# Splitting a projection step around the values, and adding a bias one unit later, in a fused cross-attention and FFN kernel

## The chip, the cores and the metric

The kernel runs on one core of a Trainium2 chip. The metric is the device time of one execution in microseconds (us). Five engines work on it side by side, each with its own queue in order: TensorE (PE in the profile, with its weight loads as PEld), VectorE (DVE), ScalarE (ACT), GpSimd (POOL) and SyncE (SP), which only issues DMAs here. Engines wait for one another by semaphores.

## The reference

Inputs are x and ctx of shape (4, 1024, 512), the projection weights of an attention with 16 heads of 32 columns, their biases, and three weight matrices of a gated feed-forward block that is computed with fake quantisation.

```
q  = layernorm(x) @ Wq + bq;  k = ctx @ Wk + bk;  v = ctx @ Wv + bv      # 16 heads of 32
scores = q k^T / sqrt(32), masked:
    image rows (the first 768) attend within their own block of 256
    text rows (the last 256) attend to all image columns, causally to text columns
x1  = x + softmax(scores) @ v @ Wo + bo
xq  = int8 fake quantisation of layernorm(x1), one scale for the whole tensor
h   = silu(xq @ quant(w_gate)^T) * (xq @ quant(w_up)^T)
out = x1 + quantised(h) @ quant(w_down)^T
```

All is fp32 to the outside; the attention's products are fp32 and the feed-forward's are bf16 of integer values.

## The kernel before, in words

The attention comes first (about 887 us), then the feed-forward block (about 250 us). The change is in the attention alone.

Each batch has four blocks of 256 queries: three image blocks and one text block. The unit of work is one block, one group of four heads and one block of 256 keys: a class `Unit`. An image block has 4 units (one part each); a text block has 16, with four parts per group. That makes 112 units. A loop over n takes them in a software pipeline written out by hand, and the order of instructions on PE, DVE, ACT and POOL is the order of this code (`manual_schedule`). Iteration n holds, for TensorE:

- `maxima`: the scores s of unit n, two PSUM tiles of two banks each, from which VectorE takes maxima;
- `large`: one projection step (`big_step`, a part of a q, k or v projection: names pp_q, pp_kv, pv) or one step of the output's projection (`step_output`, name po). A step is four products over the 128-row parts of the contraction, each in four column groups of 32 (`column_groups`). It writes one bank of a pool with one buffer (`ps_mm`, tag mm), which must be emptied before the next step: by ScalarE for pp and pv, by VectorE for po (`Output.take`);
- `weights` of unit n - 5 (`T_LAG`): the shifted scores t into two PSUM tiles, and two exp of ScalarE, one for each tile, into pT (two buffers). On POOL follow the causal mask (`affine_select`) and the running sums sp of pT over keys;
- `values` of unit n - 6 (`V_LAG`): pT times v into av; after a block's last part also the sums, sp times ones, into the same bank (L548), whose result ScalarE copies out.

s and t share one pool of three buffers (`ps_sc`, tag sc). So the second tile of s takes the buffer that the first exp of the unit before has read.

Some iterations before `LATE` (n = 84) hold a second `big_step` at their end; from `LATE` on the steps are halved. Work that is to be done a little later stands in two lists: `later`, which is run in the next iteration after `large`, and `background`, of which one entry is taken in each iteration.

`Output` is the output's projection of a block. `load` fetches x into xr (two buffers) and puts `add_bias` into `later`; `add_bias` adds bo_b to it on POOL; `take` adds po to xr on VectorE, calling `add_bias` first if that has not been done, and after the second half stores xr to x1_d by a DMA that POOL issues. `tail` is the `Output` of the last block, whose `load` is called from `values_now`.

`output_bias` makes bo_b = bo + bv @ Wo once, on all partitions: `spread` copies bv over 128 columns and `product` runs four full-size products into one bank. They are called at n = 2 and n = 4.

Of the kernel before, what the change touches and what calls it, by code (L numbers as in the profile page):

```python
# [10 lines left out]
F32 = mybir.dt.float32  # L11
# [8 lines left out]
P = 128  # L20
# [22 lines left out]
def kernel(ctx: ExitStack, tc: tile.TileContext, x, kv, Wq, bq, Wk, bk, Wv, bv, Wo, bo, clip_x, clip_down, w_gate, w_up, w_down, out):  # L43
# [78 lines left out]
    with ExitStack() as actx:  # L122
# [65 lines left out]
        def output_bias():  # L188

            bvr = wk2.tile([P, NCC, P], F32, tag="wst", name="bvr", bufs=1)  # L190

            def spread():
                nc.vector.tensor_copy(bvr, bqk[:, 2 * NCC :].unsqueeze(2).to_broadcast([P, NCC, P]))

            def product():
                pb = ps_sc.tile([P, 2, 2, QB], F32, tag="sc", name="pbo").rearrange("p a b c -> p a (b c)")[:, 0, :]
                for cc in range(NCC):
                    nc.tensor.matmul(pb, bvr[:, cc, :], W["Wo"][:, cc, :], start=(cc == 0), stop=(cc == NCC - 1))
                nc.vector.tensor_tensor(bo_b, pb, bo_b, ALU.add)

            return spread, product

# [41 lines left out]
        class Job:  # L244
# [32 lines left out]
            def rows(self, dst, w, b, scale, co, parts):  # L277

                pk = bank(f"pp_{self.kind}_{self.c}_{co}_{parts[0]}").rearrange("p (a q) -> p a q", a=2)
                for a in parts:  # L280
                    for ci in range(NCC):
                        lhs = W[w][:, ci, (co + a) * P : (co + a + 1) * P]
                        column_groups(pk[:, a, :], lhs, self.T[:, ci, :], ci == 0, ci == NCC - 1)
                for a in parts:
                    bias = bqk[:, b + co + a : b + co + a + 1]
                    nc.scalar.activation(dst[:, co + a, :], pk[:, a, :], AF.Identity, bias=bias, scale=scale)

# [17 lines left out]
            def run_big(self, half=False):  # L305

                parts = (self.part,) if half or self.part else (0, 1)
                c, i = self.c, self.big
                first = parts[0] == 0
                if self.kind == "q":  # L310
                    if i == 0 and first:
                        Q[c] = qp.tile([P, NCC, QB], F32, tag="qT", name=f"qT_{c}")
                    self.rows(Q[c], "Wq", 0, QK_SCALE, 2 * i, parts)
                elif i < 2:
                    if i == 0 and first:
                        K[c] = kp.tile([P, NCC, QB], F32, tag="kT", name=f"kT_{c}")
                    self.rows(K[c], "Wk", NCC, 1.0, 2 * i, parts)
                else:
                    i -= 2
                    if i == 0 and first:  # L320
                        V[c] = kp.tile([P, 2, C], F32, tag="va", name=f"va_{c}")
                    cols = slice(parts[0] * QB, (parts[-1] + 1) * QB)
                    pv = bank(f"pv_{c}_{i}_{parts[0]}")
                    for ci in range(NCC):
                        column_groups(pv[:, cols], self.T[:, ci, i * P : (i + 1) * P], W["Wv"][:, ci, cols], ci == 0, ci == NCC - 1)
                    nc.scalar.copy(V[c][:, i, cols], pv[:, cols])
                if parts[-1] == 1:
                    self.big += 1
                    self.part = 0
                else:  # L330
                    self.part = 1
                return len(parts)

# [143 lines left out]
        def weights(u, between):  # L477
# [16 lines left out]
            pT = wk2.tile([P, 4, 2, QB], F32, tag="pT", name=f"pT_{u.n}")  # L494
            for h in range(2):
                nc.scalar.activation(pT[:, 2 * h : 2 * h + 2], prs[h], AF.Exp)  # L496
                if h == 0:
                    between()
            if diag:

                for n in range(2):
                    d = pT[:, :, n, n * P : (n + 1) * P]
                    nc.gpsimd.affine_select(out=d, in_=d, compare_op=ALU.is_ge, fill=0.0, base=0, pattern=[[0, 4], [1, P]], channel_multiplier=-1)
            u.pT = pT

            if u.direct:
                return
            if u.part == 0:
                state["sum", k.n, g] = wk2.tile([P, 4, QB], F32, tag="sp", name=f"sp_{u.n}")
            sp = state["sum", k.n, g]  # L510
            for n in range(2):
                cols = slice(P, QB) if diag and n else slice(0, QB)
                if u.part == 0 and n == 0:
                    continue
                a = pT[:, :, 0, :] if u.part == 0 else sp[:, :, cols]
                nc.gpsimd.tensor_tensor(sp[:, :, cols], a, pT[:, :, n, cols], ALU.add)  # L516

# [52 lines left out]
        class Output:  # L570
# [5 lines left out]
            def load(self):  # L576
                if self.xr is None:
                    self.xr = load_block(x_tok, self.k.c, "xr", bufs=2)
                    later.append(self.add_bias)

# [24 lines left out]
            def step(self, half=False):  # L605
                i = self.i
                cols = slice(self.part * QB, (self.part + 1) * QB) if half or self.part else slice(0, C)
                po = ps_mm.tile([P, 512], F32, tag="mm", name=f"po_{self.k.n}_{i}_{self.part}")
                for cc in range(NCC):
                    column_groups(po[:, cols], self.k.oT[:, cc, i * P : (i + 1) * P], W["Wo"][:, cc, cols], cc == 0, cc == NCC - 1)  # L610
                statistics = self.take(po, i, cols)
                if statistics is None:
                    self.part = 1
                else:
                    background.appendleft(statistics)
                    self.part = 0
                    self.i += 1

# [82 lines left out]

        def big_step(half=False):
            nonlocal at_big, spent
            j = jobs[at_big]
            spent += BIG * j.run_big(half) / 2
            rows_done[j.kind[0], j.c] = min(2 * j.big + j.part, NCC)
            if j.big == j.bigs:
                done.add((j.kind[-1], j.c))
                at_big += 1

        def advance(n):
# [23 lines left out]

        def step_output(half=False):
            outputs[0].step(half)
            if outputs[0].i == 2:
                outputs.pop(0)
                for o in outputs[:2]:  # L740
                    o.load()

# [5 lines left out]
        def large(n):  # L748

            if n < LATE:  # L750
                if outputs and (len(outputs) > 1 or spent + BIG >= target(n)):
                    step_output()
                elif can_big(n) and spent < target(n):
                    big_step()
                elif outputs:
                    step_output()
                elif can_big(n) and spent < target(n) + 3 * BIG:
                    big_step()
                else:
                    return False  # L760
            elif can_big(n):
                big_step(n < len(units))
            elif outputs:
                step_output(n < len(units))
            else:
                return False
            return True
# [49 lines left out]
        early[0] = False  # L817
        spread, product = output_bias()
        for n in range(len(units) + V_LAG):
            previous = units[n - 1] if 0 < n <= len(units) else None  # L820
            if n < len(units):
# [6 lines left out]
                if u.part == u.parts - 1:  # L828
                    minus_maxima(u)
            if n in (2, 3, 4):  # L830
                (spread, sigmoids, product)[n - 2]()
            f = background.popleft() if background and n > 0 else None
            if f is not None and f.__name__ in ("deviation", "apply", "quantise"):
                f()
                f = background.popleft() if background and f.__name__ == "quantise" else None
            full = large(n)
            fs = list(later)
            later.clear()
# [5 lines left out]
            def shifts_of_previous():  # L844
                if previous is not None and previous.part == previous.parts - 1:
                    shifts(previous)

            def weights_now():
                if T_LAG <= n < len(units) + T_LAG:
                    weights(units[n - T_LAG], shifts_of_previous)  # L850
                else:
                    shifts_of_previous()

            def values_now():
# [4 lines left out]
                if u.part == u.parts - 1 and u.g == 0:  # L859
                    while len(outputs) >= OUTS:  # L860
                        step_output()
                if u is units[-4]:
                    tail.load()
                return values(u)

            if full:
                weights_now()
                ends = values_now()
            else:
                ends = values_now()  # L870
                weights_now()
            if n == len(units) + V_LAG - 2:
# [332 lines left out]
```

## Time and profile before

| what | value |
|---|---|
| median of 3 runs | 1138.64 us (1138.23 to 1140.09) |
| the profiled execution's own time | 1139.15 us |
| its span, first to last instruction | 1137.4 us |
| mean granted TensorE clock | 0.992 of full speed |
| PE busy | 1116.0 us, 98% of the span |
| DVE, ACT, POOL busy | 784.9, 500.1, 551.5 us |
| HBM over the span | 92 GB/s |

How to read it: the busy time of an engine is the union of its instructions' spans. Ends of matmuls are modelled, so a stall of a fraction of a microsecond inside a group of matmuls shows only in the distance from one start to the next. In a timeline line the columns are start, duration, engine, line, operation, what it writes and reads, shapes, count, and in brackets the idle time before it with what ended it.

### The profile page before, as it was taken

The numbers are of one execution on the slowest core, as the hardware profiler recorded it, in microseconds if no ns is written. First come the engines' busy times: TensorE is split into PE (matmuls) and PEld (weight loads), VectorE is DVE, ScalarE is ACT, GpSimd is POOL, SyncE is SP. The second block draws the span as 40 slices with busy tenths as digits, with TensorE's granted clock in tenths as the row PEclk, the third lists the DMA queues.
The fourth block names the chain that finished last, engine by engine and source line by source line (L and its number), as shares of the span: only waits on it lengthen the run. The fifth ranks groups of instructions, "written<-read, shape, count | busy, mean of one in ns | idle before, by whom it ended". The sixth has DMA issues, their size and how long they took to land.

```text
span 1137.4 us, 31369 instructions
## 1 busy us (share of the span) xinstructions
PE 1116.0 (98%) x13811; PEld 562.5 (49%) x13833; DVE 784.9 (69%) x979; ACT 500.1 (44%) x700; POOL 551.5 (48%) x618
## 2 busy tenths in 40 slices
PE   9999999999999999999999999998999899998998
PEld 5545545455545445454545455555554344444344
DVE  2545776766577857567777765875667788877887
ACT  3234433343444424344433445543333465553553
POOL 1224556577664567775556568657753222110110
PEclk9999999999999999999999999999999899999999
DMA  8342213133222222331312122111311599320895
GB/s 260 109 123 74 62 43 108 47 88 93 80 62 76 79 84 63 95 101 34 92 67 73 56 76 73 37 49 27 106 61 62 164 291 268 69 38 28 290 386 194
DMA packets 117201, 119.09 MB, mean 105 GB/s; under 512 B 55548, under 2 KB 86536, under 8 KB 115656
## 3 DMA queue, kind: packets, MB, share of 16 engines
q1 hardware_dynamic: 111104, 83.26, 26.3%
q0 software_dynamic: 5648, 33.30, 7.6%
q8 instruction: 108, 1.77, 0.7%
q10 hardware_dynamic: 312, 0.53, 0.2%
q14 instruction: 29, 0.24, 0.1%
HBM read 71.57 MB, written 33.29 MB: 92 GB/s over the span
## 4 chain that ended last, share of the span: by engine, by line
PE 91%; DVE 3%; DMA 2%; POOL 2%; ACT 1%; issue 1%; DVEq 0%; POOLq 0%; ACTq 0%
PE pv L219 10%; PE po L219 9%; PE pp_kv L219 9%; PE pp_q L219 9%; PE av L530 9%; PE t L491 8%; PE pg L1045 7%; PE pu L1045 7%; PE s L439 6%; PE s L428 5%; PE t L486 3%; PE av L548 3%; PE pd L1148 2%; DMA xt<-x_d 2%; POOL sp L516 2%
## 5 line engine op out<-in xcount | busy, mean ns | idle before, releaser
L496 ACT ACTIVATE pT<-t 128x1024 f32<-128x1024 f32 x224 | 217.1, 1021 | 190.2 <-PE t L491 160.1
L516 POOL TENSOR_TENSOR sp<-sp,pT 128x1024 f32<-128x1024 f32 x86 | 191.7, 2229 | 39.1 <-ACT pT L496 35.6
L450 DVE TENSOR_REDUCE nmh<-s 128x2 f32<-128x1024 f32 (+1 forms) x128 | 145.3, 1156 | 67.3 <-PE s L439 65.1
L516 POOL TENSOR_TENSOR sp<-pT 128x1024 f32<-128x1024 f32 x59 | 139.9, 2372 | 87.9 <-ACT pT L496 87.7
L432 DVE TENSOR_REDUCE nmh<-s 128x4 f32<-128x1024 f32 x96 | 112.8, 1216 | 97.7 <-PE s L428 95.5
L219 PE MATMUL pp_q<-qT,Wq_sb 128*32 128x256 f32 x2048 | 119.3, 383 | 0.0
L530 PE MATMUL av<-pT,va 128*32 128x256 f32 (+1 forms) x1792 | 116.5, 377 | 1.0 <-ACT avs L893 1.0
L219 PE MATMUL pv<-Wv_sb,kvT 128*32 128x512 f32 (+1 forms) x1088 | 116.9, 570 | 0.0
L491 PE MATMUL t<-qT,kT 32*128 32x256 f32 (+1 forms) x1792 | 113.4, 367 | 0.0
L219 PE MATMUL po<-Wo_sb,oT 128*32 128x512 f32 (+1 forms) x1120 | 110.3, 534 | 0.3
L563 DVE RECIPROCAL avs<-avs 128x256 f32<-128x256 f32 x63 | 109.8, 1742 | 0.0
L219 PE MATMUL pp_kv<-kvT,Wk_sb 128*32 128x256 f32 x1920 | 109.6, 380 | 0.0
L564 POOL TENSOR_TENSOR oT<-avs 128x256 f32<-128x256 f32 x63 | 45.9, 729 | 98.1 <-DVE avs L563 98.0
L491 PEld LDWEIGHTS t<-qT,kT 32*128 32x128 f32 x1792 | 88.3, 185 | 7.0
L1045 PE MATMUL pg<-xqT,wgT 128*128 128x512 bf16 x344 | 90.2, 382 | 1.1 <-DVE xqT L1006 0.5
L1045 PE MATMUL pu<-xqT,wuT 128*128 128x512 bf16 x345 | 90.2, 382 | 0.4
L1051 ACT ACTIVATE silu<-pg,sg 128x512 f32<-128x512 f32 x88 | 60.0, 686 | 65.6 <-PE pg L1045 63.5
L219 PEld LDWEIGHTS pp_q<-qT,Wq_sb 128*32 128x32 f32 x2048 | 63.7, 110 | 48.8 <-issue 8.7
L1072 DVE SCALAR_TENSOR_TENSOR h<-pu,su,silu 128x512 f32<-128x512 f32 x88 | 65.4, 747 | 30.9 <-PE pu L1045 28.3
L219 PEld LDWEIGHTS pp_kv<-kvT,Wk_sb 128*32 128x32 f32 x1920 | 60.1, 110 | 44.1 <-issue 5.4
L439 PE MATMUL s<-kT,qT 32*128 32x256 f32 (+1 forms) x1024 | 76.4, 387 | 3.2 <-ACT pT L496 3.2
L530 PEld LDWEIGHTS av<-pT,va 128*32 128x32 f32 x1792 | 46.8, 109 | 54.5 <-issue 23.7
(186 smaller groups left out, 1387.3 us busy)
## 6 DMA issues: line engine op xcount, KB each, us to landing
xt<-x_d SPq DMA_DIRECT2D x16, 1024.0 KB, 6.4
h<-h_d POOLq DMA_DIRECT2D x3, 2816.0 KB, 13.6
xb<-in_x_dram SPq DMA_DIRECT2D x16, 512.0 KB, 3.7
xr<-in_x_dram SPq DMA_DIRECT2D x16, 512.0 KB, 3.7
x_d<-xr POOLq DMA_DIRECT2D x16, 512.0 KB, 3.9
spread_kv<-in_ctx_dram SPq DMA_DIRECT2D x60, 128.0 KB, 2.7
xn_d<-xb SPq DMA_DIRECT2D x15, 512.0 KB, 3.3
spread_q<-xn_d SPq DMA_DIRECT2D x60, 128.0 KB, 2.7
```

Source lines behind the costliest of these rows:

```text
L219: nc.tensor.matmul(out[rows_of(j)], lhs[:, rows_of(j)], rhs, start=start, stop=stop, tile_position=(0, j * D), skip_group_check=True)
L432: nc.vector.tensor_reduce(nmh[:, h, :, :, 0], prs[h], AX.X, ALU.max, negate=True)
L439: nc.tensor.matmul(prs[j // 2][:, j % 2, kk, :w], q[rows_of(j), g, i * P : (i + 1) * P], K[k.keys[2 * half + kk]][rows_of(j), g, :w], star ...
L450: nc.vector.tensor_reduce(nmh[:, h, :, i, half], s[:, :, :n], AX.X, ALU.max, negate=True)
L491: nc.tensor.matmul(prs[j // 2][:, j % 2, n, cols], kc[rows_of(j), g, n * P : (n + 1) * P], q[rows_of(j), g, cols], start=False, stop=(n == 1))
L496: nc.scalar.activation(pT[:, 2 * h : 2 * h + 2], prs[h], AF.Exp)
L516: nc.gpsimd.tensor_tensor(sp[:, :, cols], a, pT[:, :, n, cols], ALU.add)
L530: nc.tensor.matmul(av[rows_of(j), 0, cols], va[:, n, g * P + j * D : g * P + (j + 1) * D], u.pT[:, j, n, cols], start=(u.part == 0 and n = ...
L563: nc.vector.reciprocal(avs[:, 1, :], avs[:, 1, :])
L1045: nc.tensor.matmul(ps, w[:, cc, ic * P : (ic + 1) * P], qT[:, cc, :], start=(cc == 0), stop=(cc == NCC - 1))
L1051: nc.scalar.activation(s, pg, AF.Silu, scale=sg[:, ic : ic + 1])
L1072: nc.vector.scalar_tensor_tensor(h[:, ic, :], pu, su[:, ic : ic + 1], s, ALU.mult, ALU.mult)
```

## The change

It has four parts.

1. A step of a projection now returns its last product and the emptying of its bank as two functions (`rest`) in place of running them. `finish` runs them at once, or, when `rests` is true, keeps them in `late_rest`. In an iteration before `LATE` with text values that have no sums to follow (a part other than the last), with no second `big_step` to come, the last product runs behind `values`, then the bank is emptied, and only then comes the second exp, which `weights` now returns as `second_half` together with the mask and the sums. In every other iteration `complete` runs the rest directly behind the step, as before.
2. bo_b: bv is placed in the first of 32 columns of a zeroed tile; the four products are four column tiles that write a quarter of the partitions each; ScalarE copies the bank to SBUF, and one unit later (`total`, n = 5) a product by ones adds the partitions up.
3. `add_bias` goes through `later` twice, so it runs one unit later.
4. `tail.load` is called one unit earlier (`units[-5]`).

The diff, cut to its core:

```diff
         def output_bias():
-            bvr = wk2.tile([P, NCC, P], F32, tag="wst", name="bvr", bufs=1)
+            bvr = wk2.tile([P, NCC, D], F32, tag="wst", name="bvr", bufs=1)
+            parts = wk2.tile([P, C], F32, tag="sp", name="bo_parts")
             def spread():
-                nc.vector.tensor_copy(bvr, bqk[:, 2 * NCC :].unsqueeze(2).to_broadcast([P, NCC, P]))
+                nc.vector.memset(bvr, 0.0)
+                nc.vector.tensor_copy(bvr[:, :, 0:1], bqk[:, 2 * NCC :].unsqueeze(2))
             def product():
...
                 for cc in range(NCC):
-                    nc.tensor.matmul(pb, bvr[:, cc, :], W["Wo"][:, cc, :], start=(cc == 0), stop=(cc == NCC - 1))
+                    nc.tensor.matmul(pb[rows_of(cc)], bvr[:, cc, :], W["Wo"][:, cc, :], start=True, stop=True, tile_position=(0, cc * D), skip_group_check=True)
+                nc.scalar.copy(parts, pb)
+            def total():
+                pb = ps_sc.tile([P, 2, 2, QB], F32, tag="sc", name="pbt").rearrange("p a b c -> p a (b c)")[:, 0, :]
+                nc.tensor.matmul(pb, ones, parts, start=True, stop=True)
                 nc.vector.tensor_tensor(bo_b, pb, bo_b, ALU.add)
...
             def rows(self, dst, w, b, scale, co, parts):
...
+                todo = [(a, ci) for a in parts for ci in range(NCC)]
+                for a, ci in todo[:-1]:
+                    product(a, ci)
+                return (lambda: product(*todo[-1])), take
...
-            for h in range(2):
-                nc.scalar.activation(pT[:, 2 * h : 2 * h + 2], prs[h], AF.Exp)
-                if h == 0:
-                    between()
-            if diag:
+            u.pT = pT
+            nc.scalar.activation(pT[:, :2], prs[0], AF.Exp)
+            between()
+            def second_half():
+                nc.scalar.activation(pT[:, 2:], prs[1], AF.Exp)
...
+            return second_half
...
             def load(self):
                 if self.xr is None:
                     self.xr = load_block(x_tok, self.k.c, "xr", bufs=2)
-                    later.append(self.add_bias)
+                    later.append(lambda: later.append(self.add_bias))
...
+        def finish(rest, rests):
+            late_rest.extend(rest)
+            if not rests:
+                complete()
...
-            if n in (2, 3, 4):
-                (spread, sigmoids, product)[n - 2]()
+            if n in (2, 3, 4, 5):
+                (spread, sigmoids, product, total)[n - 2]()
...
             full = large(n)
+            v = units[n - V_LAG] if V_LAG <= n < len(units) else None
+            second = n < LATE and spent + BIG < target(n)
+            if v is None or second or n >= LATE or v.part == v.parts - 1 or (jobs[at_big - 1].kind, jobs[at_big - 1].c) == ("kv", v.k.keys[v.part]):
+                complete()
...
-                if u is units[-4]:
+                if u is units[-5]:
                     tail.load()
...
-            if full:
-                weights_now()
+            if late_rest:
+                second_half = weights_now()
+                ends = values_now()
+                complete()
+                second_half()
+            elif full:
+                weights_now()()
                 ends = values_now()
             else:
                 ends = values_now()
-                weights_now()
+                weights_now()()
```

`rest` of a v step and of an output step (`Output.step`) is made in the same way; `step_output` puts the next blocks' `load` into the emptying of its last step.

More of the change, by code (lines that the diff above doesn't have):

```diff
@@ L197, in product @@
                 for cc in range(NCC):
-                    nc.tensor.matmul(pb, bvr[:, cc, :], W["Wo"][:, cc, :], start=(cc == 0), stop=(cc == NCC - 1))
+                    nc.tensor.matmul(pb[rows_of(cc)], bvr[:, cc, :], W["Wo"][:, cc, :], start=True, stop=True, tile_position=(0, cc * D), skip_group_check=True)
[3 more added lines that the diff above has]
+                nc.tensor.matmul(pb, ones, parts, start=True, stop=True)
                 nc.vector.tensor_tensor(bo_b, pb, bo_b, ALU.add)
-            return spread, product
+            return spread, product, total
         nc.gpsimd.memset(mask, 0.0)
@@ L279, in rows, with product, take @@
                 pk = bank(f"pp_{self.kind}_{self.c}_{co}_{parts[0]}").rearrange("p (a q) -> p a q", a=2)
[L280 to L286, printed above, removed]
+                def product(a, ci):
+                    lhs = W[w][:, ci, (co + a) * P : (co + a + 1) * P]
+                    column_groups(pk[:, a, :], lhs, self.T[:, ci, :], ci == 0, ci == NCC - 1)
+                def take():
+                    for a in parts:
+                        bias = bqk[:, b + co + a : b + co + a + 1]
+                        nc.scalar.activation(dst[:, co + a, :], pk[:, a, :], AF.Identity, bias=bias, scale=scale)
+                todo = [(a, ci) for a in parts for ci in range(NCC)]
+                for a, ci in todo[:-1]:
+                    product(a, ci)
+                return (lambda: product(*todo[-1])), take
             def first_rows(self):
@@ L312, in run_big @@
                         Q[c] = qp.tile([P, NCC, QB], F32, tag="qT", name=f"qT_{c}")
-                    self.rows(Q[c], "Wq", 0, QK_SCALE, 2 * i, parts)
+                    rest = self.rows(Q[c], "Wq", 0, QK_SCALE, 2 * i, parts)
                 elif i < 2:
@@ L316, in run_big @@
                         K[c] = kp.tile([P, NCC, QB], F32, tag="kT", name=f"kT_{c}")
-                    self.rows(K[c], "Wk", NCC, 1.0, 2 * i, parts)
+                    rest = self.rows(K[c], "Wk", NCC, 1.0, 2 * i, parts)
                 else:
@@ L323, in run_big, with product @@
                     pv = bank(f"pv_{c}_{i}_{parts[0]}")
-                    for ci in range(NCC):
+                    def product(ci):
                         column_groups(pv[:, cols], self.T[:, ci, i * P : (i + 1) * P], W["Wv"][:, ci, cols], ci == 0, ci == NCC - 1)
-                    nc.scalar.copy(V[c][:, i, cols], pv[:, cols])
+                    for ci in range(NCC - 1):
+                        product(ci)
+                    rest = (lambda: product(NCC - 1)), (lambda: nc.scalar.copy(V[c][:, i, cols], pv[:, cols]))
                 if parts[-1] == 1:
@@ L331, in run_big @@
                     self.part = 1
-                return len(parts)
+                return len(parts), rest
         background = deque()
@@ L494, in weights @@
             pT = wk2.tile([P, 4, 2, QB], F32, tag="pT", name=f"pT_{u.n}")
-            for h in range(2):
-                nc.scalar.activation(pT[:, 2 * h : 2 * h + 2], prs[h], AF.Exp)
-                if h == 0:
-                    between()
-            if diag:
-                for n in range(2):
[L502 to L516, printed above, removed]
+            u.pT = pT
[3 more added lines that the diff above has]
+                nc.scalar.activation(pT[:, 2:], prs[1], AF.Exp)
+                if diag:
+                    for n in range(2):
+                        d = pT[:, :, n, n * P : (n + 1) * P]
+                        nc.gpsimd.affine_select(out=d, in_=d, compare_op=ALU.is_ge, fill=0.0, base=0, pattern=[[0, 4], [1, P]], channel_multiplier=-1)
+                if u.direct:
+                    return
+                if u.part == 0:
+                    state["sum", k.n, g] = wk2.tile([P, 4, QB], F32, tag="sp", name=f"sp_{u.n}")
+                sp = state["sum", k.n, g]
+                for n in range(2):
+                    cols = slice(P, QB) if diag and n else slice(0, QB)
+                    if u.part == 0 and n == 0:
+                        continue
+                    a = pT[:, :, 0, :] if u.part == 0 else sp[:, :, cols]
+                    nc.gpsimd.tensor_tensor(sp[:, :, cols], a, pT[:, :, n, cols], ALU.add)
+            return second_half
         def values(u):
@@ L608, in step, with product, take @@
                 po = ps_mm.tile([P, 512], F32, tag="mm", name=f"po_{self.k.n}_{i}_{self.part}")
-                for cc in range(NCC):
+                last = cols.stop == C
+                def product(cc):
                     column_groups(po[:, cols], self.k.oT[:, cc, i * P : (i + 1) * P], W["Wo"][:, cc, cols], cc == 0, cc == NCC - 1)
[L611 to L617, printed above, removed]
+                def take():
+                    statistics = self.take(po, i, cols)
+                    if last:
+                        background.appendleft(statistics)
+                for cc in range(NCC - 1):
+                    product(cc)
+                self.part = 0 if last else 1
+                self.i += last
+                return (lambda: product(NCC - 1)), take
         quantised = [False]
@@ L700, with big_step @@
         rows_done = {}
-        def big_step(half=False):
+        def big_step(half=False, rests=False):
             nonlocal at_big, spent
             j = jobs[at_big]
-            spent += BIG * j.run_big(half) / 2
+            parts, rest = j.run_big(half)
+            spent += BIG * parts / 2
             rows_done[j.kind[0], j.c] = min(2 * j.big + j.part, NCC)
@@ L709, in big_step, with complete @@
                 at_big += 1
+            finish(rest, rests)
+        late_rest = []
+        def finish(rest, rests):
+            late_rest.extend(rest)
+            if not rests:
+                complete()
+        def complete():
+            for f in late_rest:
+                f()
+            late_rest.clear()
         def advance(n):
@@ L734, with step_output, take @@
         outputs = []
-        def step_output(half=False):
-            outputs[0].step(half)
+        def step_output(half=False, rests=False):
+            rest = outputs[0].step(half)
             if outputs[0].i == 2:
                 outputs.pop(0)
-                for o in outputs[:2]:
-                    o.load()
+                def take():
+                    rest[1]()
+                    for o in outputs[:2]:
+                        o.load()
+                finish((rest[0], take), rests)
+            else:
+                finish(rest, rests)
         def finished(k):
@@ L751, in large @@
                 if outputs and (len(outputs) > 1 or spent + BIG >= target(n)):
-                    step_output()
+                    step_output(rests=True)
                 elif can_big(n) and spent < target(n):
-                    big_step()
+                    big_step(rests=True)
                 elif outputs:
-                    step_output()
+                    step_output(rests=True)
                 elif can_big(n) and spent < target(n) + 3 * BIG:
-                    big_step()
+                    big_step(rests=True)
                 else:
@@ L761, in large @@
             elif can_big(n):
-                big_step(n < len(units))
+                big_step(n < len(units), True)
             elif outputs:
-                step_output(n < len(units))
+                step_output(n < len(units), True)
             else:
@@ L817 @@
         early[0] = False
-        spread, product = output_bias()
+        spread, product, total = output_bias()
         for n in range(len(units) + V_LAG):
@@ L849, in weights_now @@
                 if T_LAG <= n < len(units) + T_LAG:
-                    weights(units[n - T_LAG], shifts_of_previous)
-                else:
-                    shifts_of_previous()
+                    return weights(units[n - T_LAG], shifts_of_previous)
+                shifts_of_previous()
+                return lambda: None
             def values_now():
```

## The prediction

> **What bounds the kernel now.** I read the page first, then TensorE's waits, then the timeline of single units, since 98% busy hides stalls inside groups.
>
> ```profile
> span 1137.4 us, 31369 instructions
> PE 1116.0 (98%) x13811; PEld 562.5 (49%) x13833; DVE 784.9 (69%) x979; ACT 500.1 (44%) x700; POOL 551.5 (48%) x618
> PE 91%; DVE 3%; DMA 2%; POOL 2%; ACT 1%; issue 1%; DVEq 0%; POOLq 0%; ACTq 0%
> ```
>
> TensorE sets the time: 98% busy, 91% of the chain of waits. So each edit is worth what it takes from or adds to TensorE's queue. The waits name two large stalls:
>
> ```profile
> PE s L439 <- ACT pT L496: 3.2, 1, 3.2
> PE av L548 <- POOL sp L516: 1.5, 1, 1.5
> ```
>
> Small stalls are in no list, because ends are modelled. They show in the distance between starts. Timeline of PE for a text unit whose values have no sums, with ScalarE's exp, then an image unit with sums:
>
> ```profile
> 222.72 1.03 PE L491 MATMUL t<-qT,kT 32*128 32x256 f32 x16
> 223.69 1.07 PE L530 MATMUL av<-pT,va 128*32 128x256 f32 x16
> 224.69 1.38 PE L439 MATMUL s<-kT,qT 32*128 32x256 f32 x16
> 226.00 1.29 PE L219 MATMUL pp_q<-qT,Wq_sb 128*32 128x256 f32 x20
> ...
> 223.86 1.94 ACT L496 ACTIVATE pT<-t 128x1024 f32<-128x1024 f32 x2 [0.64 <-POOL nm L466]
> ...
> 308.42 1.07 PE L530 MATMUL av<-pT,va 128*32 128x256 f32 x16
> 309.30 0.61 PE L548 MATMUL av<-sp,ones 128*32 128x256 f32 x8
> 309.85 1.15 PE L428 MATMUL s<-kT,qT 32*128 32x256 f32 x16
> 310.92 1.49 PE L219 MATMUL pv<-Wv_sb,kvT 128*32 128x512 f32 x12
> ```
>
> The same 16 score records take 226.00 - 224.69 = 1.31 us without sums and 310.92 - 309.85 = 1.07 with them. Scores and weights share three PSUM buffers, so the second half of s takes the buffer that the first exp empties: that exp begins 0.17 after t's end and runs about 1 us, but s is there 1.00 after t's end. The sums (0.55) would have filled the time. So a unit without sums loses about 0.24 us. This is the stall that the moved product can fill.
>
> **The change part by part** (TensorE's time; minus is gain).
>
> *1. The last product behind the values.* In the changed kernel's order of instructions 26 steps do this: 10 in each of the texts of batches 0 and 1, 6 in batch 2; 14 pp steps, 10 pv, 2 po. Elsewhere the last product follows its step as before. No matmul is added. The quarter moved takes 3.59/8 = 0.45 (pp) or 3.57/4 = 0.89 us (pv, po), over the 0.24 needed. Adding s's excess over 1.08 (0.86 for the masked quarter, which has fewer columns) in just these 26 units of the timeline gives 2.33 + 2.33 + 1.37 = 6.0 us: the ceiling.
>
> *Its new wait.* ScalarE now does first exp, waits for the last product, empties the bank, does the second exp. Queued behind that wait: the second exp, later ScalarE copies, and through them POOL's sums. With t's end at 0: av 0.89, product 0.45, 0.14 to wake ScalarE (a step ending at 229.59 was emptied from 229.73), emptying 0.84 (pp), second exp ends at about 3.24 against 2.13 before. t's end is itself 0.45 earlier, so the exp is 0.66 later. For pv (0.89, copy 0.58) it is about 0.42. POOL mostly absorbs this: it idles about 2 us before a unit's sums. Who is late: where the weights were of a text's last part, the next unit's L548 reads the sums at once.
>
> ```profile
> 233.97 3.73 POOL L516 TENSOR_TENSOR sp<-sp,pT 128x1024 f32<-128x1024 f32 x2
> ...
> 238.15 0.61 PE L548 MATMUL av<-sp,ones 128*32 128x256 f32 x8
> ```
>
> The sums end at 237.70: 0.45 of slack. Five pp steps stand there (slack 0.40 to 0.47), with 0.42 to 0.66 more delay and the gained 0.18 to 0.26 pulling L548 forward: waits of 0.3 to 0.5 each, about 2.1 together, of which 0.3 hides a stall of the next s (1.39 at 238.70). The bank itself is free at 2.4, against the next step's start at 2.53; only before a masked quarter (2.31) does TensorE wait 0.07, three times. The last of the 26 feeds the 1.5 us wait for sums in the list (POOL works without a gap from 679.24 to 689.9): 0.42 later there, and TensorE 0.23 sooner, so 0.65 is lost. Sum: -6.0 + 2.1 - 0.3 + 0.2 + 0.65 = **-3.4**. The po steps empty on VectorE; their store's issue on POOL now waits for that, but t is 0.9 earlier there, so the sums end about where L548 needs them: nothing.
>
> A rule speaks against splitting a step: the Trainium skill, "TensorEngine Tiling (Array Packing)", Key Properties, says that changing the tiling mode drains TensorE. The trace has it: L548 behind av costs nothing extra, while going on to s costs 0.55 against 0.43 for L548 into a projection (100.25 to 100.68), so 0.11 a change. If the split added two changes, 26 x 0.22 = 5.7 us would eat part 1. But av and the product both use 32-column tiles, so the count of changes stays, and I charge none.
>
> *2. bo_b from four column tiles and a matmul by ones.*
>
> ```profile
> 57.79 3.70 PE L198 MATMUL pbo<-Wo_sb,bvr 128*128 128x512 f32 x8
> ```
>
> Starts give 61.42 - 57.79 = 3.63 us. Four 32-column products run side by side: L219's 32 such records take 3.57, so 8 take 0.89. The matmul by ones is one of full size, 3.63/4 = 0.91. -3.63 + 0.89 + 0.91 = **-1.8**. ScalarE's copy (0.6, from L326) has a unit to land and VectorE's add moves a unit on; both lie under TensorE's steps. If VectorE, waiting on xb's load at 64.26, set the pace there, half is lost; if the ones matmul hides, 2.7.
>
> *3. The bias added to xr a unit later.* This concerns POOL's queue: one add behind a load.
>
> ```profile
> 770.71 2.38 POOL L584 TENSOR_TENSOR xr<-xr,bo_b 128x1024 f32<-128x1024 f32 x1 [9.25 <-DMA xr<-in_x_dram]
> ...
> 773.72 4.79 POOL L516 TENSOR_TENSOR sp<-sp,pT 128x1024 f32<-128x1024 f32 x2
> ...
> 778.54 1.94 ACT L496 ACTIVATE pT<-t 128x1024 f32<-128x1024 f32 x2 [4.18 <-POOL sp L516]
> ...
> 779.62 0.92 PE L439 MATMUL s<-kT,qT 32*128 32x256 f32 x12 [3.19 <-ACT pT L496]
> ```
>
> The add holds POOL 9.25 us; sums ready at 766 begin at 773.7, their pT buffer is free only at 778.5, the exp is late and s stalls. With the add behind these sums: sums 766.1 to 770.9, cast, add 772.0 to 774.4 (the load has landed), next sums to 779.2; the exp starts at 774.9. s loses 4.74 - 1.33 = **-3.4**. The other adds move into idle POOL time: nothing.
>
> *4. The tail.* The last adds are moved too, and tail.load comes one unit earlier, ahead of block 13's load; so 13 takes the buffer that block 15 leaves, not that of 12.
>
> ```profile
> 846.06 0.69 DVE L589 TENSOR_TENSOR xr<-po,xr 128x512 f32<-128x512 f32 x1 [3.18 <-POOL oT L564]
> ...
> 860.00 0.37 SPq L136 DMA_DIRECT2D xr<-in_x_dram  x1
> ...
> 865.60 3.62 PE L219 MATMUL po<-Wo_sb,oT 128*32 128x512 f32 x32
> ```
>
> Block 15: its add now stands behind oT and sums on POOL, which end at 846.1; the add (2.4) ends at 848.5, VectorE empties po at 849.2 instead of 846.75, and the next po, at 848.37 with one bank, waits 0.85. Block 13: its load is the one of 860.00 (0.85 later still), lands 3.66 on by the chain of waits, add 2.4, emptying 0.7: 867.6 against 865.60 + 0.85, 1.2 more. **+2.1**. Loads of this size took up to 5.0 (828.02), which would make it 3.4. [...]
>
> Sum: -3.4 - 1.8 - 3.4 + 2.1 = **-6.5**. The profiled execution took 1139.15 (span 1137.4), 0.5 over the median 1138.64; 1139.15 - 6.5 = 1132.65, put to the median: **1132.1 us**.
>
> **Rivals.**
> *The sum as worked*, 1129.5 to 1135: 0.64.
> *All cover holds*: the sums are never late and the tail costs 0.9: -6.0 - 1.8 - 3.4 + 0.9 = -10.3, 1128.3. For: POOL has idle time; against: 0.40 of slack. 0.12.
> *Half gone*: L548 waits eat all of part 1 and the load at the tail takes 5.0: -1.8 - 3.4 + 3.4 = -1.8, 1136.8. 0.13; half of it counts as no change.
> *Slower*: the wait for the last product, on ScalarE in front of the second exp. If POOL had no idle time in text units, each of 26 second exps would push the sums 0.42 (12) or 0.66 (14), 14.3 us, the two pT buffers would hand that to exp and TensorE, and nothing of part 1's gain would stay: 14.3 - 1.8 - 3.4 + 2.1 = +11, 1150. It decides when POOL's gap before the sums is under 0.66; the gaps here (2.15 at 218.87, 2.37 at 247.06) speak against. 0.11.
> *Not doing what it says*: only 26 steps are split; that is in the sum.
>
> **The numbers.** About 0.2% (2.3 us) is what a measurement of this kernel can tell from no change. Faster 0.82, same 0.08, slower 0.10. Range: part 1 from -6.0 to -1.5, part 2 from -2.7 to -0.9, part 3 from -3.6 to -3.0, tail +0.9 to +3.4: 1127.5 to 1136.7.
>
> **What would show it.** Right: s behind a late product at 1.07 instead of 1.31; no wait of s near 770; pbo near 0.9; L548 waits of 0.3 to 0.6 after a text's last part; two po groups near 850 and 866 starting late. Wrong: s still at 1.3, or gaps in front of t (exp late); POOL without idle time before its sums; tail waits of several us.

## The result, and the profile after

The changed kernel's median is 1133.01 us (1131.89 to 1135.5) beside 1138.43 us for the kernel before in the same comparison: ratio 0.9953, 95% interval 0.994 to 0.9966, or 5.4 us faster; 1132.1 was forecast. The profiled execution took 1132.74 us against 1139.15: 6.4 less, 6.5 forecast. The sum was met and two of its terms were not: part 1 gave far less than forecast, part 3 more.

The page of the changed kernel, its span, busy times and the chain by engine; then the first lines of TensorE's waits:

```profile
span 1131.0 us, 31397 instructions
PE 1107.4 (98%) x13813; PEld 553.6 (49%) x13835; DVE 784.0 (69%) x980; ACT 501.4 (44%) x701; POOL 551.7 (49%) x618
PE 84%; POOL 7%; DMA 3%; DVE 2%; ACT 2%; issue 1%; POOLq 0%; DVEq 0%; SPq 0%; ACTq 0%
```

```profile
PE av L569 <- POOL sp L535: 4.5, 8, 1.9
PE pm_h L112 <- DVE diag_h L109: 3.2, 1, 3.2
PE po L226 <- DVE xr L610: 1.8, 2, 1.2
```

TensorE still sets the end, but 7% of the chain now runs over POOL (2% before). The wait of 3.2 us of s for pT is gone. The wait for sums, 1.5 us once, is 4.5 us in eight places; L569 is L548 of before. The waits of po are the tail's.

TensorE's order repeats from run to run. So the gains and losses are read from the distance between two starts of t, numbered by the pass n of the main loop. From t of pass 17 (173.61 us in before) to t of pass 86 (693.47) lie all 26 late steps ("text"); from 100 to 102 lies the stall behind the load of xr; from 112 to 116 the tail. In us:

| kernel | median | ratio to before (95%) | text | 100 to 102 | 112 to 116 |
|---|---|---|---|---|---|
| before | 1138.43 | 1 | 519.86 | 16.22 | 23.28 |
| changed | 1133.01 | 0.9953 (0.9940 to 0.9966) | 518.60 | 10.97 | 25.29 |
| no late product | 1133.22 | 0.9952 (0.9939 to 0.9965) | 519.59 | 10.97 | 25.40 |
| second exp first | 1133.21 | 0.9950 (0.9938 to 0.9962) | 519.08 | 10.97 | 25.31 |
| late without part 3 | 1133.08 | 0.9949 (0.9936 to 0.9962) | 519.11 | 10.97 | 25.47 |
| late with part 1 only | 1130.42 | 0.9930 (0.9917 to 0.9942) | 516.97 | 10.97 | 25.27 |
| bias add alone | 1132.21 | 0.9945 (0.9930 to 0.9960) | 519.86 | 10.97 | 23.28 |
| tail as before | 1129.82 | 0.9924 (0.9908 to 0.9939) | 518.60 | 10.97 | 23.06 |
| stall filled | 1136.89 | 0.9988 (0.9976 to 1.0000) | 519.88 | 15.89 | 23.29 |
| narrower choice | 1127.92 | 0.9908 (0.9891 to 0.9924) | 516.07 | 10.97 | 23.06 |
| layer norm on VectorE | 1131.56 | 0.9939 (0.9926 to 0.9953) | 519.22 | 10.97 | 25.13 |
| narrower, no po | 1126.81 | 0.9905 (0.9888 to 0.9921) | 515.82 | 10.97 | 23.06 |
| narrower, no po, layer norm | 1126.35 | 0.9895 (0.9881 to 0.9909) | 515.96 | 10.97 | 23.06 |

The two kernels that leave TensorE's order in the text stretch as it was (bias add alone, stall filled) are within 0.02 us of before there. Outside these stretches the starts differ between runs by 2 to 3 us, at the first loads and in the last quarter of the program. Medians thus carry over 1 us of noise, the stretches hundredths. Each ratio is to runs of before in the same comparison.

For the changed kernel the stretches add up to -1.26 - 5.25 + 2.01 = -4.5 us; part 2 lies ahead of them and is worth -1.7 by its own trace (below).

### The profile page after: what moved, and what is told of

It is laid out like the page before. It is cut to its first block, busy times and chain, and to the rows that moved or that the text cites. A ratio compares the mean times of both kernels' runs of the same rounds, so it can differ in the third digit from the quotient of the medians.

```text
span 1131.0 us, 31397 instructions
## 1 busy us (share of the span) xinstructions
PE 1107.4 (98%) x13813; PEld 553.6 (49%) x13835; DVE 784.0 (69%) x980; ACT 501.4 (44%) x701; POOL 551.7 (49%) x618
## 3 DMA queue, kind: packets, MB, share of 16 engines
q8 instruction: 108, 1.77, 0.7%
## 4 chain that ended last, share of the span: by engine, by line
PE 84%; POOL 7%; DMA 3%; DVE 2%; ACT 2%; issue 1%; POOLq 0%; DVEq 0%; SPq 0%; ACTq 0%
PE pv L226 9%; PE pp_kv L226 8%; PE po L226 8%; PE pp_q L226 8%; PE av L551 8%; PE t L509 7%; PE pg L1104 7%; PE pu L1104 7%; PE s L457 5%; POOL sp L535 5%; PE s L446 4%; PE t L504 3%; PE av L569 3%; PE pd L1207 2%; DMA xt<-x_d 2%
## 5 line engine op out<-in xcount | busy, mean ns | idle before, releaser
L514 ACT ACTIVATE pT<-t 128x1024 f32<-128x1024 f32 x112 | 114.7, 1024 | 253.9 <-PE t L509 239.6
L518 ACT ACTIVATE pT<-t 128x1024 f32<-128x1024 f32 x112 | 114.3, 1020 | 0.0
```

Source lines behind the costliest of these rows:

```text
L514: nc.scalar.activation(pT[:, :2], prs[0], AF.Exp)
L518: nc.scalar.activation(pT[:, 2:], prs[1], AF.Exp)
```

## The experiments

**No late product.** In the changed kernel, the rest of each step right behind it:

```
-            if v is None or second or n >= LATE or ... :
-                complete()
+            complete()
```

> Changed kernel with every last product run right after its step, so that only parts 2 to 4 stay. Theory (part 1 gains 1.3 us net, because late POOL sums take back half of the 2.3 us that each text's scores win): +1.3 against the changed kernel's 1133.0, so about 1134.3; all L569 waits for sums back to 1.5 us in total, s in a text unit back at 1.31. Rival (the prediction's sum, part 1 worth 3.4): 1136.4. Second rival (splitting is worth nothing): 1133.0.

Measured: ratio 0.9952, not to be told from the changed kernel; text 519.59 against 518.60. Part 1 is worth 1.0 us, not 3.4. The wait for sums is back at 1.5. A further 0.27 of the gain in text stays without late products. It is the stall of s at 238.70 (1.39 by starts in before, 1.10 here): the exp ahead of it starts 0.1 us after the end of t, where in before it starts 0.4 after it, just behind sums on POOL. The bias add alone does not remove this stall; why this kernel's order does stays open.

**Second exp first.** In a late step, emptying moves behind the second exp:

```
-                complete()
-                second_half()
+                late_rest.pop(0)()
+                second_half()
+                complete()
```

> Changed kernel with second exp ahead of emptying the bank: the late product stays behind the values, ScalarE does first exp, second exp, then empties. Theory (late second exp is what makes POOL's sums late): L569 waits fall from 4.5 us in total to about 1.5, gaining 3.0; but in the 14 pp steps the bank is empty at 2.97 us after t's end (second exp to 2.13, take 0.84) where the next step starts at 2.5, so about 0.45 x 14 = 6.3 us of waits appear in front of the next step; in the 10 pv steps (2.13 + 0.58 = 2.71 against 2.85) none. Sum +3.3: 1136.3. Rival (the bank has slack, only the exp counts): -3.0, 1130.0.

Neither: text 519.08, 0.5 above the changed kernel. TensorE's waits in this run:

```profile
PE pp_q L226 <- ACT qT L295: 1.7, 4, 0.5
PE pp_kv L226 <- ACT kT L295: 1.0, 3, 0.5
PE po L226 <- ACT qT L295: 1.0, 3, 0.3
PE av L569 <- POOL sp L535: 0.9, 1, 0.9
```

Both mechanisms are there. The sums come in time (0.9 instead of 4.5), and the step behind each of the 14 late steps of Q and K waits for the bank, mostly 0.32, where 0.45 was expected. That is more than the 0.24 which a late product wins. No such wait is for the bank of a V step (va): emptying takes 0.84 for rows of Q and K and 0.59 for V.

**Late with fewer parts.** The condition for running the rest at once gets one term more, first for the 7 steps with part 3's weights, then also for the 8 with part 2's:

```
-            if v is None or second ...
+            if v is None or v.part == 2 or second ...     # without part 3
+            if v is None or v.part >= 1 or second ...     # part 1 only
```

> Changed kernel, last product not late in the 7 steps whose weights are of a text's last part (part 3). Theory (the backlog on POOL is inherited from the late unit before): the 7 steps lose 0.24 each, 1.7; about half of the added 3.0 us of L569 waits stays, since part 2's exp is still late. Sum +0.2: 1133.2. Rival (the prediction's view: only the last part's own late exp makes the sums late): L569 waits back to 1.5, -3.0 + 1.7 = -1.3: 1131.7.

> Changed kernel, last product late only in the 11 steps whose weights are of a text's part 1 (15 steps of parts 2 and 3 go back). Theory (backlog inherited over two units): L569 waits back to 1.5 us, -3.0; 15 steps lose 0.24, +3.6; sum +0.6: 1133.6. Rival (the prediction's view): the same waits as with part 3 alone taken out, so slower than that one by the 8 steps of part 2, 1.9 us: 1133.6 as well if that one is 1131.7; the two are told apart by the pair of runs: theory +0.4 between them, rival +1.9.

Part 1 only is the best of these: 2.6 us under no late product in text, 11 x 0.24, so those steps lose nothing. Without part 3 lies between theory and rival. A drop of the clock costs it 1.5 us between the t of passes 85 and 86 (last section), so the kernels are compared up to t of pass 85: there part 1 only is 2.61 ahead of no late product, with part 2 as well 2.38, the changed kernel 1.35. Both views had expected part 1 only to be the slower of the pair, by 0.4 or 1.9; it is 0.23 faster.

The 8 steps of part 2 should add 8 x 0.24 = 1.9 and instead cost 0.2, so they lose 2.1. Of this, 1.7 lies in the four passes where the delay goes on to a wait for sums (0.7 each at 292 and 504 us, 0.13 in two others), and 0.43 in the pass behind the last late V step, where t waits for VectorE. The 7 of part 3 should add 1.7 and instead cost 1.0, so they lose 2.7. The rival's waits of 1.5 are refuted (2.9 in three places). POOL's timeline of the changed kernel, then of part 1 only, shows how part 2's delay is passed on:

```profile
279.83 4.81 POOL L535 TENSOR_TENSOR sp<-sp,pT 128x1024 f32<-128x1024 f32 x2 [1.26 <-ACT pT L518]
...
286.79 0.22 POOL L379 TENSOR_SCALAR ln_t<-ln_t 128x2 f32<-128x2 f32 x1
286.97 1.22 POOL L523 TENSOR_SCALAR_AFFINE_SELECT pT<-pT 128x512 f32<-128x512 f32 x2
288.16 3.70 POOL L535 TENSOR_TENSOR sp<-sp,pT 128x1024 f32<-128x1024 f32 x2
```

```profile
279.00 4.83 POOL L535 TENSOR_TENSOR sp<-sp,pT 128x1024 f32<-128x1024 f32 x2 [0.48 <-ACT pT L518]
...
286.17 1.22 POOL L523 TENSOR_SCALAR_AFFINE_SELECT pT<-pT 128x512 f32<-128x512 f32 x2
287.37 3.73 POOL L535 TENSOR_TENSOR sp<-sp,pT 128x1024 f32<-128x1024 f32 x2
```

The first row's bracket is all of POOL's idle time: behind it sums of part 2, small casts, the layer norm, mask and sums of part 3 run without a gap to 291.86. A second exp that comes 0.83 later (279.83 against 279.00) therefore ends the sums 0.8 later. TensorE then waits; first the changed kernel, then part 1 only:

```profile
290.37 0.86 PE L551 MATMUL av<-pT,va 128*32 128x256 f32 x16
291.92 0.64 PE L569 MATMUL av<-sp,ones 128*32 128x256 f32 x8 [0.69 <-POOL sp L535]
```

```profile
290.79 0.86 PE L551 MATMUL av<-pT,va 128*32 128x256 f32 x16
291.46 0.61 PE L569 MATMUL av<-sp,ones 128*32 128x256 f32 x8
```

From the start of av to that of L569 it is 1.55 against 0.67.

**Layer norm on VectorE.** Takes the layer norm's small steps out of POOL's run:

```
-                nc.gpsimd.tensor_scalar_add(v, v, EPS)
+                nc.vector.tensor_scalar_add(v, v, EPS)      # and the six behind it
```

> Changed kernel with the seven small steps of the layer norm (mean, deviation) on VectorE instead of POOL, where they hold 2.0 us between two units' sums (285.2 to 287.2 in the changed kernel). Theory (part 1's loss is a backlog of POOL's whole busy stretch): POOL's sums there end 1.5 us or more earlier, the 0.69 us waits of L569 at 292 and 504 us are gone; each stretch gives back 0.9 (the step's loss in TensorE's order), so 1.8 together; the wait of 1.88 at 687 stays, since there the layer norm stands behind the sums; 1131.2. Rival (the wait comes from the late second exp alone, or VectorE passes its own delay on): waits of 0.5 to 0.7 stay at 292 and 504, 1133.0.

Half right: the pass with that wait loses 0.43 instead of 0.90 beside part 1 only, in both places. POOL's timeline and TensorE's of this run:

```profile
286.51 1.22 POOL L523 TENSOR_SCALAR_AFFINE_SELECT pT<-pT 128x512 f32<-128x512 f32 x2 [1.34 <-ACT pT L518]
287.70 3.73 POOL L535 TENSOR_TENSOR sp<-sp,pT 128x1024 f32<-128x1024 f32 x2
```

```profile
290.55 0.86 PE L551 MATMUL av<-pT,va 128*32 128x256 f32 x16
291.48 0.64 PE L569 MATMUL av<-sp,ones 128*32 128x256 f32 x8
```

POOL now has idle time and the mask waits for part 3's own second exp. So the 0.43 is put down to that exp, within the 0.3 to 0.5 of the prediction, and the other 0.47 to POOL's full run. The text of 519.22 again holds a drop of the clock behind t of pass 85, of 1.6 us.

**Bias add alone.** The kernel before, with

```
-                    later.append(self.add_bias)
+                    later.append((lambda: later.append(self.add_bias)) if self.k.c <= 12 else self.add_bias)
```

> Kernel before with only the bias added to xr a unit later, and that not for the last blocks (13 to 15), so that the tail is as before. Theory (the 3.2 us stall also dropped TensorE's clock, so its end costs 5.25 instead of 3.4): -5.3 near 776 us, -0.3 near 240 us: 5.6 below before. Rival (the prediction's sum: the stall's length alone): -3.4.

The stretch from 100 to 102 falls from 16.22 to 10.97: 5.25. The size is the theory's; its reason is not, as the next run shows, and the 0.3 near 240 us did not appear.

**Stall filled.** The kernel before, with TensorE kept busy in the stall:

```
+                if n == 101:
+                    filler = ps_mm.tile([P, 512], F32, tag="mm", name="filler")
+                    for _ in range(13):
+                        nc.tensor.matmul(filler.rearrange("p (a b) -> p a b", a=4), onesb, rhs, start=True, stop=True)
                 maxima(u)
```

> Kernel before with 13 idle bf16 matmuls (128x512, 2.8 us together) in front of the scores whose stall of 3.2 us stands near 776 to 780 us; the wait itself stays, TensorE is only busy in it. Theory (the stall drops the clock: granted 0.57 in the 4 us behind it, the projection step there 3.1 us instead of 1.9): with no idle time the clock stays at 1.00, the step takes 1.9, the next t comes 1.3 to 1.9 us earlier than in before: -1.6. Rival (the step is slow for another reason, or filler matmuls only cost time): 0 to +0.5.

First two windows of before (start:end, length, busy times and counts of PE, PEld, DVE, ACT, POOL, then PEclk, the granted clock, the DMA share and GB/s), across the stall and behind it, and the projection step of before behind the stall; then the filled kernel's timeline:

```profile
775.00:780.40 5.40, 2.21 (x32) 1.22 (x24) 0.00 (x0) 1.86 (x2) 5.24 (x6) 1.00 0.03 7
780.40:784.40 4.00, 4.00 (x44) 1.98 (x44) 2.69 (x4) 0.55 (x2) 3.92 (x3) 0.57 0.21 44
```

```profile
780.47 3.20 PE L219 MATMUL pp_q<-qT,Wq_sb 128*32 128x256 f32 x32
```

```profile
775.33 2.98 PE L830 MATMUL filler<-onesb 128*128 128x512 bf16 x13
778.24 1.66 PE L439 MATMUL s<-kT,qT 32*128 32x256 f32 x16
779.82 1.94 PE L219 MATMUL pp_q<-qT,Wq_sb 128*32 128x256 f32 x32
...
784.26 1.01 PE L530 MATMUL av<-pT,va 128*32 128x256 f32 x16 [1.31 <-POOL pT L503]
```

In before the mean clock over the 4 us behind the stall is 0.57 and the projection step takes 3.20; filled, it takes 1.94. From t of pass 100 the next t comes after 8.35 us instead of 9.85: the 1.5 of the theory. But av then waits 1.31 for POOL's mask, and one pass on only 0.33 is left. POOL of before says why:

```profile
779.47 4.79 POOL L516 TENSOR_TENSOR sp<-sp,pT 128x1024 f32<-128x1024 f32 x2
784.22 1.22 POOL L503 TENSOR_SCALAR_AFFINE_SELECT pT<-pT 128x512 f32<-128x512 f32 x2
```

POOL, late by its add, stops TensorE twice: in s, then in av. In before the slow clock let TensorE reach av only at 785.16, when the mask was nearly done, and so covered the second stop. So the two do not add. Against the bias add alone the filled kernel still loses 3.38 us in the first of the two passes and 1.54 in the second; what the clock adds to these 4.92 is 0.33.

**Tail as before.** The changed kernel, with the add of blocks 13 to 15 undelayed as above, and

```
-                if u is units[-5]:
+                if u is units[-4]:
                     tail.load()
```

> Changed kernel with the tail's load one unit later again (as before) and the add of blocks 13 to 15 not delayed; the rest as changed. Theory (the tail costs 2.0): the two waits of po for xr, 1.8 us in all, are gone, about 2.0 below the changed kernel: 1131.0, span 1129.0. Rival (the tail is bound by oT and POOL's sums anyway, the waits only change their name): 1133.0.

The theory holds: both waits of po are gone, 25.29 falls to 23.06, the median to 1129.82.

**Narrower choice**, three kernels. Late for Q and K rows with part 1's weights only; for V with every part, second exp ahead of emptying; the two po steps late in the first kernel and not in the others; in the third the layer norm on VectorE as well; the tail as before in all. `step_kind` names the step that `large` has run.

```
+            if v is None or (v.part >= 1 and step_kind[0] == "pp") or second ...    # no po: != "pv"
...
+                if step_kind[0] == "pv":
+                    late_rest.pop(0)()
+                    second_half()
+                    complete()
```

> Changed kernel with the late product kept where POOL can bear it: in steps of rows of Q and K only for weights of part 1 (as in the run with only part 1); for steps of V in all parts, with the second exp ahead of emptying the bank, since their bank is taken in 0.6 and is in time; for the two po steps, which VectorE empties. Tail as in the kernel before. Theory: text parts 1.6 us below the changed kernel by the narrower choice, four V steps at 0.24 and two po steps at 0.5 more, tail -2.0: 5.6 below the changed kernel, 1127.4. Rival (the V and po steps bring the backlog on POOL back): only the tail's 2.0, 1131.0.

> The narrower choice (late only with part 1's weights, and V steps in all parts with the second exp ahead of emptying), tail as before, now without the two po steps. Theory (the po step's store waits on POOL for VectorE's add, ahead of the mask and sums: sums 0.2 late at 264.6): 0.15 us gained for each of two, 0.3 in the trace, 1127.6. Rival (the po step gains the 0.26 of its s and loses nothing): 0.5 more, 1128.4.

> The same without the po steps, with the layer norm's small steps on VectorE. Theory (no wait of L569 is left that the layer norm feeds): no more than 0.2 from the kernel without this, 1127.6. Rival (POOL still sets the pace somewhere that no wait shows): 1126 or less.

All three beat both kernels. The first came out at 1127.92 (1127.4 expected; the rival's 1131.0 is refuted). Without the po steps text is 515.82, 0.25 less than with them (0.3 expected), and 2.8 under the changed kernel: 15 late steps win 3.77 over no late product, 0.25 each. The layer norm on VectorE adds 0.14 in text and 0.62 in the pass right behind it, where a t waits 0.29 for VectorE near 689; the theory's 0.2 does not hold in the trace, and the medians cannot tell, since the intervals of the three overlap. What a late V step with the exp first looks like, on TensorE and on ScalarE:

```profile
219.28 1.03 PE L509 MATMUL t<-qT,kT 32*128 32x256 f32 x16
220.24 1.07 PE L551 MATMUL av<-pT,va 128*32 128x256 f32 x16
221.13 1.04 PE L226 MATMUL pv<-Wv_sb,kvT 128*32 128x512 f32 x8
222.10 1.15 PE L457 MATMUL s<-kT,qT 32*128 32x256 f32 x16
223.17 3.01 PE L226 MATMUL pp_q<-qT,Wq_sb 128*32 128x256 f32 x52
```

```profile
220.41 1.02 ACT L514 ACTIVATE pT<-t 128x1024 f32<-128x1024 f32 x1 [4.40 <-PE t L509]
221.33 1.02 ACT L518 ACTIVATE pT<-t 128x1024 f32<-128x1024 f32 x1
222.24 0.59 ACT L344 COPY va<-pv 128x512 f32<-128x512 f32 x1
```

The bank is empty at 222.83, ahead of the next step at 223.17, and s takes 223.17 - 222.10 = 1.07. In the changed kernel, whose t starts here 0.05 later (219.33), the copy stood ahead of the second exp, which so started 3.44 us after t instead of 2.05:

```profile
222.29 0.59 ACT L344 COPY va<-pv 128x512 f32<-128x512 f32 x1 [0.80 <-PE pv L226]
222.77 1.03 ACT L518 ACTIVATE pT<-t 128x1024 f32<-128x1024 f32 x1
```

## Why the prediction was right, and where it was not

- *Part 1, gain.* Right. s behind a late product takes 1.07 or 1.08. In the three masked units it takes 1.03 where 0.86 was forecast, since the next step then waits for the bank. Over the 26 units s is 5.7 us shorter than in before (6.0 forecast). No change of tiling mode was to be charged: the 11 steps of part 1 keep their 0.24 whole.
- *Part 1, its new wait.* Mis-sized: 3.4 forecast, 1.0 left. The step that failed is "POOL mostly absorbs this". The late exps of part 3 were put at 2.0 (2.1 less 0.3, and 0.2 at the bank) and cost 2.7. Of part 2's eight only the last was charged, 0.65 at the wait for sums of 1.5; the other seven were put at nothing. The eight cost 2.1 up to pass 85, and that wait grew by a further 0.34 (1.52 with part 1 only, 1.86 without part 3). Most of it is POOL's: where it runs through two units with a layer norm or a cast between their sums, the delay reaches the next unit's sums, and TensorE arrives with the gains of two steps. The slack of 0.45 was read from one unit of before, where no delay came in from the unit ahead. What each part costs holds with the parts before it late, as here.
- *The po steps.* "Nothing" was wrong by little: in the narrower choice each is a net loss of 0.13.
- *Part 2.* Right. The bias products in the changed kernel are

```profile
57.47 1.06 PE L200 MATMUL pbo<-Wo_sb,bvr 128*32 128x512 f32 x8
58.35 7.09 PE L226 MATMUL pp_kv<-kvT,Wk_sb 128*32 128x256 f32 x128
...
66.45 1.13 PE L205 MATMUL pbt<-bo_parts,ones 128*128 128x512 f32 x2
67.50 2.78 PE L226 MATMUL pv<-Wv_sb,kvT 128*32 128x512 f32 x24
```

  By starts 0.88 and 1.05 instead of 3.63: -1.7, with -1.8 forecast (0.89 and 0.91). No run has part 2 alone. But the first t starts at 71.0 to 72.3 us in the ten kernels with part 2 and at 72.5 to 73.1 in the three without it, two groups that do not overlap, though the noise of the first loads is as large as the gain.
- *Part 3.* Right place and cause, mis-sized: 3.4 forecast, 5.25 measured. The step that failed is "s loses 4.74 - 1.33": it ended the account at the first thing that waited, and the wait of av behind it was worth another 1.5. The changed kernel's POOL does the add at 768.50 without a wait, and the mask comes 5.0 us after t of pass 100 (775.59 and 770.57), where in before it came 10.2 after it (784.22 and 773.98).
- *Part 4.* Right: +2.1 forecast, 2.01 measured against before and 2.23 against the tail as before, in the two places named:

```profile
840.48 3.64 PE L226 MATMUL po<-Wo_sb,oT 128*32 128x512 f32 x32 [0.57 <-DVE xr L610]
...
858.93 3.64 PE L226 MATMUL po<-Wo_sb,oT 128*32 128x512 f32 x32 [1.24 <-DVE xr L610]
```

  The forecast waits were 0.85 and 1.2; the passes there grew by 0.78 and 1.45.
- *The rivals.* The slower one, POOL without idle time, was real in a few stretches of each text and not in all 26 steps. "Half gone" named the right loss and left part 3 too small. "All cover holds" is refuted by the waits for sums and for xr. The lower end of the range adds up to 1127.2, not 1127.5; nothing hangs on it.

Part 1 came out 2.4 short and part 3 1.85 over, so that the total of -6.5 lay so near -6.4 is in part luck: two misses cancelled.

## What to carry to other kernels

A delay in front of an engine that is half idle on average is free only where idle time follows before the next consumer: take the slack over the engine's whole unbroken run, with the delay it inherits and the lead that the gain gives its consumer. When a stall goes, follow the late engine to the next thing it feeds, for a wait that comes second may be covered by the first. And choose by step: a split paid 0.24 us each where the bank was quickly emptied or the sums had room, and lost that and more elsewhere.

## What the hardware showed

A wait of under two microseconds can halve TensorE's clock, and not each time. The same wait for sums near 686 us was 1.86 us without part 3 and 1.88 in the changed kernel. Behind the first, s took 2.02 us instead of 1.08 by starts, and the pass 1.5 us more. Two windows of the first kernel, then of the second, columns as above, each cut where the granted clock can change:

```profile
682.92:686.33 3.41, 1.55 (x36) 0.75 (x32) 0.00 (x0) 2.00 (x3) 3.33 (x3) 1.00 0.47 110
686.33:689.74 3.41, 3.41 (x29) 1.57 (x32) 0.32 (x1) 1.70 (x3) 2.83 (x10) 0.50 0.12 26
```

```profile
682.03:685.44 3.41, 2.74 (x52) 1.40 (x44) 1.14 (x2) 1.83 (x3) 3.33 (x4) 1.00 0.29 58
685.44:688.85 3.41, 2.20 (x36) 1.26 (x40) 0.45 (x1) 1.17 (x2) 2.83 (x10) 1.00 0.35 99
```

In these profiles the granted clock is 1.00 or 0.50, and within a profile its changes lie a whole number of slots of 3.41 us apart: without part 3 it falls at 686.33 and again at 884.30, 58 such slots later. (So the 0.57 behind the stall of before is 3.41 us at 0.50 in a window of 4.) Counted back from the fall at 883.41, the changed kernel has an edge at 685.44, in the middle of its wait. So without part 3 the whole wait fell into one slot, of which TensorE worked 1.55 us, and the next slot ran at half clock. In the changed kernel the wait was shared by two slots, with 2.74 and 2.20 us of work, and the clock stayed.

The other kernels agree. A slot with 1.36 us of work (before, in the stall of 3.19) and one with 1.52 (layer norm on VectorE, a wait of 1.90) were followed by half clock; slots with 1.88 (no late product, 1.53) and 1.99 (tail as before, 1.90) were not. Counted so from 12 us on, in the feed-forward block too, all 29 falls ahead of TensorE's last product in the 13 profiles follow a slot with at most 1.69 us of work, and no slot with 1.77 or more is followed by one. That is about half a slot, worked out from these traces alone, with modelled ends of matmuls. Four slots near 1040 us, in four of the kernels, had 1.42 to 1.52 and kept the clock; why stays open. The Trainium skill, "TensorE: Matmul & The Clock Gate", HAM oscillation, warns of idle gaps over about 3.4 us; the stall of 3.19 in before fits that roughly, the 1.86 does not, and here the measurement decides. A wait of two microseconds thus cost 1.9 or 3.4, by where it lay between two edges.
